# Channel stage: three images as one stationary operand on the way back from the spectra, the second parity's rows from partition 64

## The chip, the cores and the metric

The kernel runs on one core of a Trainium2 chip. The metric is the time of one execution on the device in microseconds, taken as the median of three runs. Beside the timed runs there is one execution under the hardware profiler, and all views shown come from it. Engines are named as in the profile: PE is the matrix engine (its weight loads are listed apart as PEld), DVE the vector engine, ACT the scalar engine, POOL the GpSimd engine, SP the engine whose queue issues most DMAs.

## The reference, cut to what matters

Input and output are 32 images of 192 channels of 56 x 56 float32. Four layers are added one after the other, each to the group-normalised image: an attention, a two-way scan, a shift, and a long convolution. The last two work on each channel by itself, and they are what the channel stage computes:

```python
# layer 2: each group of 4 channels is moved by whole pixels and smoothed by a 3x3 Gaussian
x = x + _L2_conv_ref(_gn(x), L2_conv_offset)
# layer 3: circular convolution by way of the spectra, with one 55x55 filter a channel
x = x + _L3_conv_ref(_gn(x), ...)

def _L3_conv_ref(x, ...):
    ...
    xf = jnp.fft.rfft2(x, s)
    kf = jnp.fft.rfft2(k[0], s)
    y = jnp.fft.irfft2(xf * kf[None], s)
    y = y[..., Kh // 2:Kh // 2 + H, Kw // 2:Kw // 2 + W]
    return y + bias * x

def _gn(v, G=32, eps=1e-5):      # 32 groups of 6 channels, per image
    ...
    return ((g - m) / jnp.sqrt(s + eps)).reshape(v.shape)
```

## The kernel before

Four stages run one after the other: the filters and their spectra (`make_filter`), the attention image by image, the scan by pairs of images, and at the end `channel_blocks`, which takes all 32 images of one channel at a time. The change lies in that last stage, in the constants that it loads, and in the place of the filter's rows in `make_filter`.

In the channel stage the 32 images stand as 16 pairs. Images of even and odd number (two "parities") are held on two ranges of partitions: a tile `x` has on partitions 0 to 56 the 56 rows, and one row of means, of the even images, on 57 to 113 those of the odd ones, and along the free dimension 16 images x 56 columns. One DMA fills it (L1582), and 15 such tiles rotate (pool `d_x`, L1477).

The groups of six channels are pipelined: while group n is shifted and centred, group n-1 goes through its spectra. For each channel these generators run, and the loop at L1719 to L1735 steps them in a fixed order written out as a tuple (L1726 to L1729):

- `shift` (L1577, two a step for the first three steps of a group): 8 matmuls with `x` as the stationary operand and the row matrix moving (L1589), DVE scales the result into `turned` (L1596), 8 matmuls with `turned` stationary and the column matrix moving (L1607), DVE adds to `x` (L1615) and sums it (L1616). The two matrices are made on POOL for four channels at a time, one of them with a matmul (L1550).
- `centre` (L1631, two a step for the last three steps): DVE subtracts the means into `padded` (L1633), ACT squares, DVE sums (L1636). `middle` and `spread` sum over the group with small matmuls (L1624).
- `analyse` (L1644): 8 matmuls with the padded rows of four images stationary (L1757), ACT copies of the result into `y` (L1763), then in three batches a real and an imaginary matmul (`re`, `im`, L1655) and six DVE operations each, which multiply by the filter's spectrum into `real` and `imag` (L1662 to L1668).
- `synthesise` (L1671): the way back. Columns first: for each of the 16 pairs `real` and then `imag` of the pair's 2 x 42 frequencies is the stationary operand (84 x 84) and the constant `f3` moves (112 columns, L1681); four pairs share a PSUM bank, and ACT copies each bank to `z` (L1688). Then rows: the constant `f4` (84 x 114) is stationary and `z` of eight pairs moves (448 columns, L1698); DVE scales by the group's deviation (L1700) and adds to `x` (L1701). Two DMAs store the channel, one for each parity (L1704). The generator yields after each bank of columns (four times) and each half of the rows (twice).

`synthesise` of channel j runs during the step of channel j+1 under the name `ending`. The tiles `ps` are four PSUM banks shared by all of this, `re` and `im` have two banks each. The instructions of an engine run in a fixed order; the order across the generators is that of the tuple, as the tile framework's scheduler leaves it. A matmul of float32 appears in the trace as two matmuls with a weight load each.

At the stage's start, DMAs bring the offsets and the constants, DVE works out the taps of all shifts from the offsets (from L1501), and POOL builds the first matrices from them.

Of the kernel before, what the change touches and what calls it, by code (L numbers as in the profile page):

```python
# [20 lines left out]
F32 = mybir.dt.float32  # L21
# [9 lines left out]
S = 56  # L31
N = S * S
# [36 lines left out]
def _resize_matrix():  # L69
# [4 lines left out]

CHANNEL = (
    (114, (2 * 2 * NF,)), (128, (2, 2 * NF)), (84, (2, 2 * S)), (84, (2, 114)), (114, (114,)), (114, (114,)),
    (114, (114,)), (112, (112,)), (114, (2,)),
)  # L80


# [39 lines left out]
def _spectral_constants():  # L122

    R = S + 1
    u, p = np.arange(NF), np.arange(S)
    turn = 2 * np.pi / PERIOD * np.outer(p, u)
    cos, sin = np.cos(turn), np.sin(turn)
    f1 = np.zeros((2, R, 2, 2, NF))
    for s in range(2):
        f1[s, :S, s, 0], f1[s, :S, s, 1] = cos, sin  # L130
# [12 lines left out]
    f4 = np.zeros((2, NF, 2, 2, R))  # L143
    for s in range(2):
        f4[s, :, 0, s, :S], f4[s, :, 1, s, :S] = weight * cos, -weight * sin
    row = np.arange(2 * R) % R
    same = np.arange(2 * R)[:, None] // R == np.arange(2 * R)[None, :] // R
    ones = np.where(same & (row[:, None] < S), 1.0 / (GROUP * N), 0.0)
    lags = np.where(row[None, :] < S, np.eye(2 * R), np.where(same & (row[:, None] < S), -1.0, 0.0))
    in_rows = same & (row[:, None] < S) & (row[None, :] < S)  # L150
    diff_y = np.where(in_rows, row[None, :] - row[:, None], 1e6)
# [3 lines left out]
    at_rows = np.stack([np.concatenate([col, [0, 0]]), row], 1)  # L155
    return {
        "f1": f1.reshape(2 * R, -1),
        "f2": f2.reshape(128, 2, -1),
        "f3": f3.reshape(2 * NF, 2, -1),
        "f4": f4.reshape(2 * NF, 2, -1),  # L160
        "ones_rows": ones,
        "lags": lags,
        "diff_y": diff_y,
        "diff_x": diff_x,
        "at_rows": at_rows,
    }
# [42 lines left out]
def make_filter(ctx: ExitStack, tc: tile.TileContext, a, consts, filt, spectra, beside):  # L209
# [84 lines left out]
        nc.sync.dma_start(out=filt[t * T : (t + 1) * T], in_=out[:, t])  # L294


    NI, PR = 16, 2 * (S + 1)
# [9 lines left out]
    for c0 in range(0, C, 2 * NI):  # L307
        t = padded[c0 // (2 * NI) % 2]
        for i in range(2):
            nc.sync.dma_start(  # L310
                out=t[(S + 1) * i : (S + 1) * i + KS, :, 0:KS],
                in_=filt[c0 + i : c0 + 2 * NI : 2].rearrange("q (a b) -> a q b", b=KS),
            )
# [12 lines left out]
        nc.sync.dma_start(out=spectra[:, c0 : c0 + 2 * NI], in_=g)  # L326
# [1136 lines left out]
def channel_blocks(ctx: ExitStack, tc: tile.TileContext, a, k, x2, rs2, spectra, out):  # L1463
# [5 lines left out]

    nc = tc.nc
    NB = out.shape[0]
    NI, NG = NB // 2, NB // 4
    PR = 2 * (S + 1)
# [25 lines left out]
    nc.vector.tensor_scalar(off, off, -(2.0**21), 2.0**21, ALU.max, ALU.min)  # L1501
    rnd = cp.tile([PR, NP, 2], F32, name="rnd", tag="rnd")
# [29 lines left out]
    def matrices(n):  # L1532
# [4 lines left out]
        for d, diff in ((1, diff_y), (0, diff_x)):  # L1537
# [9 lines left out]
            nc.gpsimd.tensor_tensor(mat, t[0], t[2], ALU.add)  # L1547
            if d == 1:
                ps = pp.tile([128, BANK], F32, name="ps", tag="ps", bufs=4)
                nc.tensor.matmul(ps[:PR, :PR], lags, mat, start=True, stop=True)  # L1550
                mat = wp.tile([r, m], F32, name="mat2", tag="mat2", bufs=3)
                nc.vector.tensor_copy(mat, ps[:PR, :PR])
            got.append(mat)
        made.clear()
        made[n] = got
# [2 lines left out]
    def psum():  # L1558
        return pp.tile([128, BANK], F32, name="ps", tag="ps", bufs=4)
# [17 lines left out]
    def shift(q, j):  # L1577

        c = q.n * GROUP + j
        rows, cols = matrices(c // 4)  # L1580
        x = xp.tile([PR, NI, S], F32, name="x", tag="x")
        nc.sync.dma_start(out=x, in_=x2[c].rearrange("s h g w -> (s h) g w"))  # L1582
        flat = x.rearrange("p g w -> p (g w)")
        turned = wp.tile([2 * S, NG, 2, S + 1], F32, name="turned", tag="turned")
        for g0 in range(0, NG, 4):
            n = min(4, NG - g0)
            ps = psum()
            for g in range(n):
                nc.tensor.matmul(  # L1589
                    ps[: 2 * S, g * PR : (g + 1) * PR],  # L1590
                    flat[:, (g0 + g) * 2 * S : (g0 + g + 1) * 2 * S],
                    rows,
                    start=True,
                    stop=True,
                )
            nc.vector.tensor_tensor(  # L1596
                turned[:, g0 : g0 + n].rearrange("p g s h -> p (g s) h"),
                ps[: 2 * S, : n * PR].rearrange("p (g h) -> p g h", h=S + 1),
                _bc(q.scale[:, j, g0 : g0 + n].rearrange("p g s -> p (g s)"), [2 * S, 2 * n, S + 1]),
                ALU.mult,  # L1600
            )
        yield
        for g0 in range(0, NG, 4):
            n = min(4, NG - g0)
            ps = psum()
            for g in range(n):
                nc.tensor.matmul(  # L1607
                    ps[:PR, g * 2 * S : (g + 1) * 2 * S],
                    turned[:, g0 + g].rearrange("p s h -> p (s h)"),
                    cols,  # L1610
                    start=True,
                    stop=True,
                )
# [57 lines left out]
    def synthesise(q, j, product):  # L1671

        c = q.n * GROUP + j
        real, imag = product
        z = wp.tile([84, NI, 2, S], F32, name="z", tag="z")
        for i0 in range(0, NI, 4):
            n = min(4, NI - i0)
            ps = psum()
            for i in range(n):
                for m, part in enumerate((real, imag)):  # L1680
                    nc.tensor.matmul(  # L1681
                        ps[:84, i * 2 * S : (i + 1) * 2 * S],
                        part[:, i0 + i].rearrange("p s u -> p (s u)"),
                        f3[:, m, :],
                        start=(m == 0),
                        stop=(m == 1),
                    )
            nc.scalar.copy(  # L1688
                z[:, i0 : i0 + n].rearrange("p g m w -> p (g m w)"), ps[:84, : n * 2 * S]
            )  # L1690
            yield
        x = q.x[j]
        for i0 in range(0, NI, 8):
            n = min(8, NI - i0)
            ps = psum()
            got = ps[:PR, : n * S].rearrange("p (g w) -> p g w", w=S)
            for m in range(2):
                nc.tensor.matmul(got, f4[:, m, :], z[:, i0 : i0 + n, m, :], start=(m == 0), stop=(m == 1))  # L1698
            o = wp.tile([PR, 8, S], F32, name="o", tag="o")[:, :n]
            nc.vector.tensor_tensor(o, got, _bc(q.rs[:, i0 : i0 + n], [PR, n, S]), ALU.mult)  # L1700
            nc.vector.tensor_tensor(x[:, i0 : i0 + n], x[:, i0 : i0 + n], o, ALU.add)  # L1701
            yield
        for s in range(2):
            nc.sync.dma_start(  # L1704
                out=out[s::2, c].rearrange("b h w -> h b w"), in_=x[(S + 1) * s : (S + 1) * s + S]
            )

    def centres(q, j):
# [187 lines left out]
```

## Time and profile before

| what | us |
|---|---|
| median of 3 runs (lowest, highest) | 12293.82 (12292.39, 12298.46) |
| the profiled execution | 12294.66 |
| its span, first to last instruction | 12292.8 |
| channel stage, first to last instruction | 8371.8 to 12292.8 |
| of 8500 to 9500: PE, DVE, ACT busy | 987.7, 869.4, 360.3 |
| L1681, columns back (`real`; `imag`): instructions, busy | 6144, 1090.9; 6144, 1089.5 |
| L1698, rows back: instructions, busy | 1536, 608.8 |
| L1607 / L1589 / L1757: instructions each | 3072 / 3072 / 3072 |
| L1624, L1550: instructions | 768, 96 |
| L1688, ACT's copies of `z`: count, busy, mean | 768, 405.6, 0.528 |
| L1700 / L1701, DVE: count, mean | 384, 0.612 / 384, 0.623 |

The busy time of a group is the union of its instructions' durations. A matmul's duration runs from its start to the modelled end of its result, and the next one begins long before that; two neighbouring groups therefore overlap, and the cost of a matmul on PE is read from the distance between starts. The wait at the start of a line stands in brackets, with what ended it.

### The profile page before, as it was taken

The numbers are of one execution on the slowest core, as the hardware profiler recorded it, in microseconds if no ns is written. First come the engines' busy times: TensorE is split into PE (matmuls) and PEld (weight loads), VectorE is DVE, ScalarE is ACT, GpSimd is POOL, SyncE is SP. The second block draws the span as 40 slices with busy tenths as digits, with TensorE's granted clock in tenths as the row PEclk, the third lists the DMA queues.
The fourth block names the chain that finished last, engine by engine and source line by source line (L and its number), as shares of the span: only waits on it lengthen the run. The fifth ranks groups of instructions, "written<-read, shape, count | busy, mean of one in ns | idle before, by whom it ended". The sixth has DMA issues, their size and how long they took to land. (4 is left out here: it accounts for less than half of the span.)

```text
span 12292.8 us, 164375 instructions
## 1 busy us (share of the span) xinstructions
PE 11329.2 (92%) x62734; PEld 7107.7 (58%) x62734; DVE 10836.4 (88%) x15489; ACT 6205.0 (50%) x11808; POOL 2250.7 (18%) x2228
## 2 busy tenths in 40 slices
PE   7999999999999999788888888888999999999999
PEld 3555555655555555333333333336777777777777
DVE  6888888888888887999999999997888888888888
ACT  3555555555555554566666666663333333333333
POOL 0000000000000000655555555551000000000000
PEclk9999999999999999999999999999999999999999
DMA  2111111111111111244344433442111111111111
GB/s 69 40 42 46 52 41 40 40 40 40 40 40 40 42 50 44 75 103 100 95 97 103 101 94 97 103 101 65 44 41 45 41 44 42 44 42 44 42 43 29
DMA packets 930055, 719.69 MB, mean 59 GB/s; under 512 B 770325, under 2 KB 807236, under 8 KB 920124
## 3 DMA queue, kind: packets, MB, share of 16 engines
q1 hardware_dynamic: 919020, 683.39, 21.7%
q10 hardware_dynamic: 10240, 25.70, 0.8%
q8 instruction: 500, 8.19, 0.3%
q14 instruction: 295, 2.42, 0.1%
HBM read 403.47 MB, written 240.65 MB: 52 GB/s over the span
## 5 line engine op out<-in xcount | busy, mean ns | idle before, releaser
L572 DVE SCALAR_TENSOR_TENSOR o<-v_a,att_w,o 128x896 f32<-128x896 f32 (+1 forms) x1024 | 1053.8, 1029 | 418.6 <-ACT v_a L546 291.5
L1763 ACT COPY y<-ps 64x252 f32<-64x252 f32 (+1 forms) x2376 | 808.2, 340 | 1135.0 <-PE ps L1757 1104.8
L1681 PE MATMUL ps<-fixed,real 84*84 84x112 f32 x6144 | 1090.9, 259 | 0.0
L1681 PE MATMUL ps<-fixed,imag 84*84 84x112 f32 x6144 | 1089.5, 259 | 0.0
L1688 ACT COPY z<-ps 84x448 f32<-84x448 f32 x768 | 405.6, 528 | 1218.5 <-PE ps L1681 1217.0
L1086 POOL MEMSET f<- 128x1 f32 x96 | 8.9, 99 | 4726.3 <-DMA st_c<-st 4721.3
L1681 PEld LDWEIGHTS ps<-fixed,real 84*84 84x84 f32 x6144 | 784.0, 153 | 134.2 <-issue 95.8
L1681 PEld LDWEIGHTS ps<-fixed,imag 84*84 84x84 f32 x6144 | 763.8, 153 | 0.0
L1079 ACT ACTIVATE q<-q 128x784 f32<-128x784 f32 x384 | 328.2, 855 | 802.5 <-DVE q L1074 633.1
L834 PE MATMUL ps<-sq,fixed 128*128 128x392 f32 x512 | 297.3, 743 | 428.6 <-ACT sq L1157 428.6
L572 DVE SCALAR_TENSOR_TENSOR o<-v_c,att_w,o 128x448 f32<-128x448 f32 (+1 forms) x1024 | 635.0, 620 | 5.1
L585 PE MATMUL ps<-xs_a,gk_a 128*98 128x448 f32 (+1 forms) x1536 | 637.1, 495 | 0.0
L589 ACT ACTIVATE pr<-ps,low 98x896 f32<-98x896 f32 (+1 forms) x384 | 352.3, 918 | 559.9 <-DVE low L587 559.9
L586 PE MATMUL ps<-xs_c,gk_c 125*98 125x448 f32 (+1 forms) x1536 | 631.6, 492 | 0.0
L1547 POOL TENSOR_TENSOR mat<-tap,tap 114x114 f32<-114x114 f32 x96 | 40.8, 425 | 3166.1 <-PE ps L1607 2313.2
L677 PE MATMUL ps<-gq_a,xs_a 128*112 128x294 f32 x1792 | 602.8, 417 | 19.2 <-DVE pq L682 19.2
L1698 PE MATMUL ps<-z,fixed 84*114 84x448 f32 x1536 | 608.8, 539 | 0.0
L834 PE MATMUL ps<-x,weights 128*128 128x392 f32 x1536 | 577.4, 519 | 27.5 <-DVE bv L1108 14.2
L678 PE MATMUL ps<-gq_c,xs_c 125*112 125x294 f32 x1792 | 594.5, 412 | 0.0
L1655 PE MATMUL re<-y,fixed 128*84 128x420 f32 (+1 forms) x1152 | 532.3, 543 | 8.7 <-ACT y L1763 7.6
L1655 PE MATMUL im<-y,fixed 128*84 128x420 f32 (+1 forms) x1152 | 526.9, 538 | 0.0
L690 ACT ACTIVATE pq<-pq 112x1176 f32<-112x1176 f32 x224 | 265.3, 1184 | 498.9 <-DVE pq L682 376.0
(367 smaller groups left out, 29245.2 us busy)
## 6 DMA issues: line engine op xcount, KB each, us to landing
x<-x SPq DMA_DIRECT2D x576, 392.0 KB
x<-x SPq DMA_DIRECT2D x512, 196.0 KB
x<-x SPq DMA_DIRECT2D x192, 399.0 KB
out_x<-x SPq DMA_DIRECT2D x384, 196.0 KB
x<-in_x SPq DMA_DIRECT2D x32, 1568.0 KB
x<-x SPq DMA_DIRECT2D x32, 1568.0 KB
x<-in_x SPq DMA_DIRECT2D x64, 392.0 KB
rd<-rd ACTq DMA_DIRECT2D x128, 196.0 KB
```

The costliest lines, as they stand in the source:

```text
L572: nc.vector.scalar_tensor_tensor(dst, tap(i), dww[:, t, i : i + 1], dst, ALU.mult, ALU.add)
L585: mm(ps[P2, h, :n], g[:, cols], xs_a[j][:, px], start=True, stop=False)
L586: mm(ps[P2, h, :n], gk_c[0:KC, 2 * j + h, cols], xs_c[j][0:KC, px], start=False, stop=True)
L589: nc.scalar.activation(pr[:, :, :n], ps[P2, :, :n], AF.Exp, bias=low[:, j, p : p + 1], accum_out=sums[:, j, p : p + 1])
L677: mm(ps[:SUB, i, :HA], xs_a[j][:, px], g, start=True, stop=False)
L678: mm(ps[:SUB, i, :HA], xs_c[j][0:KC, px], gq_c[0:KC, 2 * j + (q + i) // ns], start=False, stop=True)
L834: mm(out, aa, srcs[t][h], start=True, stop=False)
L1655: nc.tensor.matmul(ps[:, : n * 84], f2[:, i, :], y[:, i0 : i0 + n].rearrange("p g s u -> p (g s u)"), start=True, stop=True)
L1681: nc.tensor.matmul(ps[:84, i * 2 * S : (i + 1) * 2 * S], part[:, i0 + i].rearrange("p s u -> p (s u)"), f3[:, m, :], start=(m == 0), stop= ...
L1688: nc.scalar.copy(z[:, i0 : i0 + n].rearrange("p g m w -> p (g m w)"), ps[:84, : n * 2 * S])
L1698: nc.tensor.matmul(got, f4[:, m, :], z[:, i0 : i0 + n, m, :], start=(m == 0), stop=(m == 1))
L1763: nc.scalar.copy(y[64 * m : 64 * m + 64, 2 * g0 + i : 2 * (g0 + n) : 2], got[64 * i : 64 * i + 64, :, :, m, :])
```

## The change

`synthesise` now takes three images at a time as the stationary operand of the columns: `real` and `imag` are read as one run of 32 x 42 frequencies and cut into pieces of 126, ten whole ones and a last one of 84 (two images). That gives 11 x 2 matmuls in place of 16 x 2, in banks of 4, 4 and 3 pieces. `z` has 126 partitions and 11 pieces.

The rows that come next have to sort three images of a piece back to the parities. Two consecutive pieces hold six images, that is three pairs: the first pair comes from the even piece (its images 0 and 1), the third from the odd piece (its images 1 and 2), the middle pair from the even piece's last and the odd piece's first image. `f4` therefore has four blocks of columns: two of 121 columns for the first and third pairs, and two of 64 columns for the middle pair, whose two matmuls write partitions 0 to 63 and 64 to 127 of the same bank. The 16 pairs are taken as 9 and 7; the seventh of the second lot comes from the last piece alone.

For that the second parity's rows start at partition 64 instead of 57, everywhere: `PR` is 64 + 57 = 121, the constants are laid out anew, and `x` is loaded by two DMAs, one for each parity. The `x` tiles are now fixed (15 of them), cleared once in partitions 32 to 63, and so are the two `turned` tiles, whose parities lie 64 columns apart. The row matrix keeps 114 columns, so the moving operand of L1589 is as wide as before.

`synthesise` yields five times a channel instead of six.

```diff
+PR = 64 + S + 1
...
-    xp = ctx.enter_context(tc.tile_pool(name="d_x", bufs=15))
...
+    shifted = [cp.tile([PR, NI, S], F32, name=f"x{i}", tag=f"x{i}") for i in range(15)]
+    for t in shifted:
+        nc.vector.memset(t[32:64], 0.0)
+    sides = [cp.tile([2 * S, NG, 2, 64], F32, name=f"turned{i}", tag=f"turned{i}") for i in range(2)]
+    for t in sides:
+        nc.vector.memset(t[:, :, :, S + 1 : 64], 0.0)
...
-        x = xp.tile([PR, NI, S], F32, name="x", tag="x")
-        nc.sync.dma_start(out=x, in_=x2[c].rearrange("s h g w -> (s h) g w"))
+        x, turned, W = shifted[c % len(shifted)], sides[c % 2], 2 * (S + 1)
+        for s in range(2):
+            nc.sync.dma_start(out=x[64 * s : 64 * s + S + 1], in_=x2[c, s])
...
-                    turned[:, g0 + g].rearrange("p s h -> p (s h)"),
+                    turned[:, g0 + g].rearrange("p s h -> p (s h)")[:, 0:PR],
...
-        z = wp.tile([84, NI, 2, S], F32, name="z", tag="z")
-        for i0 in range(0, NI, 4):
-            n = min(4, NI - i0)
+        parts = [t.rearrange("p g s u -> p (g s u)") for t in product]
+        z = wp.tile([126, NT, 2, S], F32, name="z", tag="z")
+        for i0 in range(0, NT, 4):
+            n = min(4, NT - i0)
             ps = psum()
+            rows = []
             for i in range(n):
+                at = 126 * (i0 + i)
+                r = min(126, NB * 42 - at)
+                rows.append(r)
...
+                        ps[:r, i * 2 * S : (i + 1) * 2 * S], part[:, at : at + r], f3[:, m, :], start=(m == 0), stop=(m == 1)
...
+            full = rows.count(126)
+            for r, i, k in ((126, 0, full), (rows[-1], full, n)):
+                if i < k:
+                    nc.scalar.copy(
+                        z[:r, i0 + i : i0 + k].rearrange("p g m w -> p (g m w)"), ps[:r, i * 2 * S : k * 2 * S]
+                    )
             yield
...
-        for i0 in range(0, NI, 8):
-            n = min(8, NI - i0)
+        for p0 in range(0, NI, 9):
+            n = min(9, NI - p0)
+            k0, k = 2 * (p0 // 3), n // 3
             ps = psum()
...
+            ev, od = z[:, k0 : k0 + 2 * k : 2], z[:, k0 + 1 : k0 + 2 * k : 2]
+            if k > 0:
+                sums += [
+                    ((got[:PR, 0 : 3 * k : 3], f4[:, :, 0:PR], ev),),
+                    ((got[:PR, 2 : 3 * k : 3], f4[:, :, PR : 2 * PR], od),),
+                    (
+                        (got[0:64, 1 : 3 * k : 3], f4[:, :, 2 * PR : 2 * PR + 64], ev),
+                        (got[64:128, 1 : 3 * k : 3], f4[:, :, 2 * PR + 64 : 2 * PR + 128], od),
+                    ),
+                ]
+            left, at = n - 3 * k, k0 + 2 * k
+            if left > 0:
+                r = min(126, NB * 42 - 126 * at)
+                sums.append(((got[:PR, 3 * k : 3 * k + 1], f4[:r, :, 0:PR], z[:r, at : at + 1]),))
...
+            for beside in sums:
+                for m in range(2):
+                    for to, w, src in beside:
+                        nc.tensor.matmul(to, w[:, m], src[:, :, m], start=(m == 0), stop=(m == 1))
```

More of the change, by code (lines that the diff above doesn't have):

```diff
@@ L142, in _spectral_constants @@
     weight = np.where(u == 0, 1.0, 2.0)[:, None] / PERIOD**2
[L143 to L151, printed above, removed]
+    f4 = np.zeros((3, NF, 2, 2 * PR + 128))
+    for i, c in ((0, 0), (1, 64), (1, PR), (2, PR + 64), (2, 2 * PR), (0, 2 * PR + 64)):
+        f4[i, :, 0, c : c + S], f4[i, :, 1, c : c + S] = weight * cos, -weight * sin
+    parity, row = np.arange(PR) // 64, np.arange(PR) % 64
+    same = parity[:, None] == parity[None, :]
+    ones = np.where(same & (row[:, None] < S) & (row[None, :] <= S), 1.0 / (GROUP * N), 0.0)
+    lags = np.where(row[None, :] < S, np.eye(PR), np.where(same & (row[:, None] < S) & (row[None, :] == S), -1.0, 0.0))
+    to = np.arange(2 * R)
+    in_rows = (parity[:, None] == to[None, :] // R) & (row[:, None] < S) & (to[None, :] % R < S)
+    diff_y = np.where(in_rows, to[None, :] % R - row[:, None], 1e6)
     col = np.arange(2 * S) % S
@@ L1549, in matrices @@
                 ps = pp.tile([128, BANK], F32, name="ps", tag="ps", bufs=4)
-                nc.tensor.matmul(ps[:PR, :PR], lags, mat, start=True, stop=True)
+                nc.tensor.matmul(ps[:r, :m], lags, mat, start=True, stop=True)
                 mat = wp.tile([r, m], F32, name="mat2", tag="mat2", bufs=3)
-                nc.vector.tensor_copy(mat, ps[:PR, :PR])
+                nc.vector.tensor_copy(mat, ps[:r, :m])
             got.append(mat)
@@ L1673, in synthesise @@
         c = q.n * GROUP + j
-        real, imag = product
-        z = wp.tile([84, NI, 2, S], F32, name="z", tag="z")
-        for i0 in range(0, NI, 4):
-            n = min(4, NI - i0)
+        parts = [t.rearrange("p g s u -> p (g s u)") for t in product]
+        z = wp.tile([126, NT, 2, S], F32, name="z", tag="z")
+        for i0 in range(0, NT, 4):
+            n = min(4, NT - i0)
             ps = psum()
+            rows = []
             for i in range(n):
-                for m, part in enumerate((real, imag)):
+                at = 126 * (i0 + i)
+                r = min(126, NB * 42 - at)
+                rows.append(r)
+                for m, part in enumerate(parts):
@@ L1695, in synthesise @@
             ps = psum()
[L1696 to L1701, printed above, removed]
+            got = ps[:, : n * S].rearrange("p (g w) -> p g w", w=S)
@@ new lines, in synthesise @@
+            sums = []
+            ev, od = z[:, k0 : k0 + 2 * k : 2], z[:, k0 + 1 : k0 + 2 * k : 2]
[8 more added lines that the diff above has]
+                ]
@@ new lines, in synthesise @@
+            left, at = n - 3 * k, k0 + 2 * k
+            if left > 0:
+                r = min(126, NB * 42 - 126 * at)
+                sums.append(((got[:PR, 3 * k : 3 * k + 1], f4[:r, :, 0:PR], z[:r, at : at + 1]),))
+            if left == 2:
+                r = NB * 42 - 126 * (at + 1)
+                sums.append(
+                    (
+                        (got[0:64, 3 * k + 1 : 3 * k + 2], f4[:, :, 2 * PR : 2 * PR + 64], z[:, at : at + 1]),
+                        (got[64:128, 3 * k + 1 : 3 * k + 2], f4[:r, :, 2 * PR + 64 : 2 * PR + 128], z[:r, at + 1 : at + 2]),
+                    )
+                )
@@ L1704, in synthesise @@
             nc.sync.dma_start(
-                out=out[s::2, c].rearrange("b h w -> h b w"), in_=x[(S + 1) * s : (S + 1) * s + S]
+                out=out[s::2, c].rearrange("b h w -> h b w"), in_=x[64 * s : 64 * s + S]
             )
```

39 lines of the change are left out of this document (17 added, 22 removed).

## The prediction

> **What bounds the kernel now.** I read first the slices of the page, to see which stage the change lies in and which engine fills it.
>
> ```profile
> PE   7999999999999999788888888888999999999999
> DVE  6888888888888887999999999997888888888888
> PEclk9999999999999999999999999999999999999999
> ```
>
> The channel stage is the last 13 slices (8371.8 us to the end at 12292.8). There PE is at 9 in every slice, DVE at 8, and the granted clock stays full. A busy PE row counts pipelined matmuls, so I went on to windows over single channels (one window runs from one channel's first L1757 to the next one's; columns are length, then busy us of PE, PEld, DVE, ACT, POOL, then clock, DMA share, GB/s).
>
> ```profile
> 9720.91:9737.29 16.38, 16.17 (x101) 11.69 (x100) 14.64 (x25) 8.10 (x18) 0.00 (x0) 1.00 0.21 51
> 9656.91:9680.07 23.16, 22.93 (x167) 18.39 (x166) 19.08 (x34) 6.20 (x16) 3.21 (x6) 1.00 0.14 36
> ```
>
> Of a group's six channels, three also carry two `shift`s (about 23.2 us), three carry two `centre`s (17.6, 16.4 and 17.7 us). PE leaves 0.2 us idle. The timeline of the short channel shows what PE does with it.
>
> ```profile
> 9720.91 2.44 PE L1757 MATMUL ps<-fixed,padded 114*128 114x168 f32 x16
> 9723.56 0.94 PE L1655 MATMUL re<-y,fixed 128*84 128x420 f32 x2 [0.21 <-ACT y L1763]
> 9734.28 3.17 PE L1698 MATMUL ps<-z,fixed 84*114 84x448 f32 x8
> 9737.29 1.88 PE L1757 MATMUL ps<-fixed,padded 114*128 114x168 f32 x12
> ```
>
> Matmuls follow each other without a hole, but for a wait of some 0.4 us on ACT's copies of `y`. So what counts is not a matmul's duration (latency is in it) but its spacing, start to start. L1698: 3.01 us for 8, 0.376 each. L1757: (2.44 - 0.31)/15 = 0.142 each for 168 moving columns.
>
> ```profile
> 9665.87 0.35 PE L1681 MATMUL ps<-fixed,real 84*84 84x112 f32 x2
> ...
> 9667.98 0.35 PE L1681 MATMUL ps<-fixed,imag 84*84 84x112 f32 x2
> 10004.01 1.76 PE L1607 MATMUL ps<-mat,turned 112*114 112x112 f32 x16
> 9705.98 1.37 PE L1624 MATMUL ps<-sums,fixed 114*114 114x16 f32 x12 [0.21 <-ACT y L1763]
> ```
>
> L1681: 22 starts in 2.11 us, 0.096 each. L1607 moves the same 112 columns against 114 stationary ones instead of 84: (1.76 - 0.26)/15 = 0.100. L1624 moves only 16 against 114 and needs as long: (1.37 - 0.25)/11 = 0.10. So there are two floors, one by moving columns and one by stationary columns, and at 114 stationary ones the second gives 0.100. I take it in proportion: 0.106 at 121 columns, 0.1105 at 126.
>
> **The change, part by part.** Every matmul written is two of the trace (L1681: 32 a channel in the code, 12288 = 64 x 192 in the page).
>
> Way back, columns (L1681). 64 instructions of 0.096 are 6.14 us a channel. After it, ten threes at 126 columns are 40 instructions, the last piece (84) four: 40 x 0.1105 + 4 x 0.096 = 4.80. That is -1.34 us a channel, -257 us over 192. At 0.100 (the row of 114) it would be -338, at 0.112 (the same proportion carried to 128) -246.
>
> The Trainium skill, "TensorE: Matmul & The Clock Gate", section LDWEIGHTS, speaks against counting by matmuls saved: loading time goes with the stationary columns. It gives columns/1.2 ns, 0.095 at 114, where L1607 and L1624 show 0.100; by its figure 126 columns would be 0.105 and 121 0.101, and the whole sum, an estimate from that page, some 70 us lower than mine.
>
> Way back, rows (L1698). 8 instructions of 0.376 are 3.01 us. After it the first nine pairs take 4 instructions for the lower images and 4 for the third ones (121 stationary, 168 moving, 0.142), and 4 steps of two 64-column matmuls side by side for the middle image that straddles two threes. The second seven have 112 moving columns, where the 121 stationary ones decide: 12 x 0.106 (4 of them for the image left over) and 4 steps at 0.096. The channel stage has no such halves today; the attention stage has, and shows both gain and price.
>
> ```profile
> 2515.59 0.92 PE L544 MATMUL ps<-xs_a,att_w 128*128 128x448 f32 x2
> 2516.34 0.92 PE L545 MATMUL ps<-xs_c,att_c 65*128 65x448 f32 x2
> 2517.19 0.97 PE L551 MATMUL ps<-xs_a,att_w 128*64 128x448 f32 x4
> 2517.99 0.92 PE L553 MATMUL ps<-xs_c,att_c 65*64 65x448 f32 x4
> 2518.84 1.02 PE L834 MATMUL ps<-o,att_w 128*128 128x448 f32 x2
> ```
>
> The halves' eight matmuls take 1.65 us, four steps of 0.376 (1.50) and 0.15 more: two run side by side at the price of one. The two of L545 ahead of them take 0.85, where those of L544 take 0.75. A stretch of halves so costs 0.24 us on top. First part: 12 x 0.142 + 0.24 = 1.94; second: 12 x 0.106 + 4 x 0.096 + 0.24 = 1.90; together 3.84, +0.83 us a channel, +160 us.
>
> The Trainium skill, "TensorEngine Tiling (Array Packing)", sections Overview and Key Properties, promises up to twofold for 64 columns and says that a change of mode drains the engine, without a price. By the twofold alone, the sum would be 2 x 0.24 x 192 = 92 us lower; the row above is what the drain costs, and I keep it.
>
> Rows from partition 64. L1607's stationary operand grows from 114 to 121 columns: 16 a channel x 0.006 x 192 = +18 us. L1624: 768 x 0.006 = +5. L1589 (112 stationary) and L1757 (128) keep their columns; contracting 121 rows instead of 114 shows in no spacing (84, 112 and 128 rows all follow columns). DVE and ACT work on more partitions with as many elements, so their times stay. ACT's copies of `z` fall from 4 x 0.528 to two of those and two shorter ones; ACT is idle half the time, worth nothing. SP issues one more load a channel (0.28 us each) on a queue that is otherwise idle for most of a channel; the buffers and how far ahead they are loaded stay at 15.
>
> New clearing at the stage's start: 15 DVE memsets of 896 columns and two short ones, ahead of the offsets' arithmetic in DVE's order.
>
> ```profile
> 8374.77 0.21 DVE L1501 TENSOR_SCALAR off<-off 114x96 f32<-114x96 f32 x1 [2.89 <-DMA off<-in_L_conv_offset]
> L906 DVE MEMSET wogs<- 128x128 f32 x1 | 0.2, 165 | 0.1
> ```
>
> 128 columns take 165 ns, one column 59 (L1496), so 896 take about 0.81 us: 15 x 0.81 + 0.3 = 12.4 us, less the 2.9 in which DVE waits there anyway: +9.5 us, on the chain that builds the first matrices while PE waits. At worst 12.4, at best 0 if the first group catches up.
>
> Order. With one `yield` fewer, the first half of the rows now stands right after the columns, ahead of the second `shift` of a channel, and its two DVE operations (0.68 and 0.62) ahead of L1596 on DVE. In the order in which the changed program's instructions stand, L1607 then follows L1589 directly in the second shift channel of a group, as it does here:
>
> ```profile
> 9671.95 1.74 PE L1589 MATMUL ps<-mat,x 114*112 114x114 f32 x16
> 9672.93 0.63 DVE L1596 TENSOR_TENSOR turned<-ps,scale 112x456 f32<-112x456 f32 x1 [1.75 <-PE ps L1589]
> 9673.72 1.02 PE L1607 MATMUL ps<-mat,turned 112*114 112x112 f32 x8
> ```
>
> Today L1596 starts 0.98 us after L1589 and DVE has been idle for 1.75. After it, DVE gets the rows' result at 0.2 and is done at about 1.4; `turned` comes 0.42 us later, and PE waits for it: 0.42 x 32 groups = +13 us. In the other two shift channels a L1655 pair (0.85 or 1.7) stands between and hides it. In the centre channels DVE needs (16.06 + 14.64 + 17.20)/3 = 15.97 us of PE's 17.2; PE's 17.2 falls to about 16.7, so DVE still fits, though with 0.7 us to spare instead of 1.2.
>
> Sum: -257 + 160 + 18 + 5 + 9.5 + 13 = -51.5 us. The profiled execution took 12294.66 (span 12292.8 and 1.9 around it); 12294.7 - 51.5 = 12243, and as the median lies 0.8 lower, **12242 us** (-0.42%).
>
> **The rivals.** *Wide operands load unseen.* If 126 and 121 columns cost no more than 84, the spacing is 0.096 throughout: Z falls by another 40 x 0.0145 x 192 = 111, the rows by 12 x 0.010 x 192 = 23, the +23 vanish: 12085 us. For it: nothing beyond a queue that loads ahead. Against it: L1624, 0.10 for 16 moving columns.
>
> *DVE's idle time stays.* If DVE cannot give up its 1.2 us of idle a centre channel (in-order waits on `re`, `im` with two buffers each), the three centre channels keep their length, and 96 x 0.45 = 43 us of the gain are lost: 12285. For it: 17.20 of 17.66 busy in the third one. Against it: those windows leave 1.7 in the other two.
>
> *PE waits for DVE at every shift (slower).* Place: L1607 behind L1596, now behind the rows' two operations or a backlog of L1655's six. Price 0.58 us (a whole 1.3 us less the 0.72 that L1589 covers), twice a shift channel, 192 times: 111, less the 13 counted: 12340. It decides once L1655 no longer stands between or is itself late; a mean of 0.27 us a channel eats the whole gain. For it: L1589 waits already cost 0.2 at L1607. Against: the order above.
>
> *The halves do not run side by side.* Then 4 x 0.142 + 4 x 0.096 = 0.95 more a channel: 12425. For it: here the two read alternate threes of one tile. Against it: the row of L551.
>
> **How the numbers follow.** Forecast 0.58 (its own range 12205 to 12280: from 0.107 a wide matmul and no clearing that shows, to 0.112 and twice the waits), unseen loads 0.08, DVE's idle stays 0.16, slower 0.14, halves in turn 0.04. About 0.2% (25 us) is what a measurement of this kernel tells from no change, so faster means under 12269: 0.08 and six sevenths of the forecast, 0.58; within: the rest of it and DVE's idle, 0.24; slower 0.18. Range 12160 to 12325, which takes in the -338 of the columns: it leaves out the unseen loads, the halves in turn and part of the slower case.
>
> **What would show it.** Spacing of the 126-column matmuls near 0.110 (0.096 proves the first rival); the 64-column ones in pairs some 7 ns apart with about 0.1 us lost before and 0.15 in and after them; short channels at 15.9 and shift channels at 22.9; L1607's wait in one shift channel of three. The prediction is wrong if L1607 or L1655 wait on DVE in most channels, or if a stretch of halves costs other than 0.24.

## The result, and the profile after

| | us |
|---|---|
| before, median of 5 runs, the three above among them (lowest, highest) | 12293.82 (12292.39, 12298.80) |
| after, median of 5 runs (lowest, highest) | 12358.94 (12357.29, 12364.13) |
| ratio, with its 95% interval | 1.0052 (1.0038 to 1.0067) |
| span of the profiled execution, before and after | 12292.8 and 12357.1 |

The changed kernel is slower by 65 us, where 51.5 less were forecast, and the time lies outside the range. The first part of the page (busy us of each engine, share of the span, instructions) already says of what kind the loss is:

```profile
PE 11290.6 (91%) x64270; PEld 7234.4 (59%) x64270; DVE 10832.5 (88%) x15506; ACT 6092.2 (49%) x11808; POOL 2263.1 (18%) x2228
```

PE was busy for 11329.2 us before. It now has 39 us less to do in a span that is 64 us longer, and DVE as much as before (10836.4). So the work as a whole did not become dearer; the engines wait. The slices don't show it: their rows of PE, DVE and PEclk are the same, digit by digit. So I took the distance from one channel's first analysis matmul (L1757, now L1801) to the next one's, medians over the stage, by the place of the channel in two successive groups of six (channels 1 to 3 shift, 4 to 6 centre; channel 1 also finishes the group before):

| us | 1 | 2 | 3 | 4 | 5 | 6 | 1 | 2 | 3 | 4 | 5 | 6 |
|---|---|---|---|---|---|---|---|---|---|---|---|---|
| before | 23.03 | 23.17 | 23.26 | 17.58 | 16.38 | 17.66 | 23.25 | 23.20 | 23.22 | 17.58 | 16.38 | 17.66 |
| after | 25.22 | 23.04 | 22.79 | 17.29 | 16.01 | 17.98 | 27.09 | 22.78 | 22.77 | 17.28 | 16.01 | 17.98 |

Eight of the twelve are shorter, by 0.13 to 0.47. Channel 1 is longer by 2.19 and 3.84, channel 6 by 0.32. With 16 such pairs of groups: these eight -2.8 x 16 = -45, channel 1 +6.0 x 16 = +96, channel 6 +0.32 x 32 = +10, and the first matmul of the stage starts 9.4 later (8395.33 for 8385.97); together about +71 by medians, where the spans differ by 64. The same by windows of the changed kernel, one channel each (length, then busy us of PE, PEld, DVE, ACT, POOL, clock, DMA share, GB/s): channels 5, 6, 1 and 2.

```profile
9746.56:9762.57 16.01, 15.80 (x110) 12.29 (x110) 14.30 (x25) 6.49 (x17) 0.00 (x0) 1.00 0.21 52
9762.57:9780.56 17.99, 16.85 (x121) 13.33 (x120) 15.22 (x26) 7.44 (x18) 0.00 (x0) 1.00 0.18 46
9780.56:9807.65 27.09, 24.07 (x179) 19.46 (x178) 22.60 (x39) 6.98 (x19) 4.08 (x5) 1.00 0.15 37
9807.65:9830.43 22.78, 22.60 (x175) 18.98 (x174) 18.89 (x33) 5.64 (x16) 2.32 (x5) 1.00 0.14 37
```

In the third line PE is idle for 3.0 us, DVE for 4.5 and ACT for 20. No engine is full there; they wait for each other. The timeline of that channel's start shows in what order. (Line numbers are now those of the changed kernel: square L1647, its sum L1648, centring L1645, rows L1744 and L1745, copies of `y` L1807, small sums L1636.)

```profile
9779.45 0.67 DVE L1745 TENSOR_TENSOR x<-x,o 121x504 f32<-121x504 f32 x1
9780.05 1.08 DVE L1645 TENSOR_TENSOR padded<-x,mean 121x896 f32<-121x896 f32 x1
9780.56 1.96 PE L1801 MATMUL ps<-fixed,padded 121*128 121x168 f32 x12
...
9781.64 0.67 DVE L1675 TENSOR_TENSOR a<-im,g 84x504 f32<-84x504 f32 x1
9781.70 2.62 ACT L1807 COPY y<-ps 64x252 f32<-64x252 f32 x7 [7.14 <-PE ps L1801]
9783.24 0.84 PE L1801 MATMUL ps<-fixed,padded 121*128 121x168 f32 x4 [0.72 <-ACT y L1807]
...
9784.23 0.95 ACT L1647 ACTIVATE sq<-padded 121x896 f32<-121x896 f32 x1
...
9785.21 1.08 DVE L1648 TENSOR_REDUCE sums<-sq 121x16 f32<-121x896 f32 x1 [2.90 <-ACT sq L1647]
...
9786.21 0.93 DVE L1676 TENSOR_TENSOR real<-a,a 84x504 f32<-84x504 f32 x1
9786.35 0.38 PE L1636 MATMUL ps<-sums,fixed 121*121 121x16 f32 x2 [0.25 <-DVE sums L1648]
...
9787.07 0.67 DVE L1678 TENSOR_TENSOR a<-re,g 84x504 f32<-84x504 f32 x1
...
9787.79 0.94 PE L1667 MATMUL re<-y,fixed 128*84 128x420 f32 x2 [1.06 <-DVE a L1678]
```

The group's last centring ends at 9781.13; the rows of the channel before (L1744, L1745) now stand ahead of it on DVE. Its square could start then; ACT is idle. But in ACT's order seven copies of the next channel's `y` stand ahead of it, and the first of these starts at 9781.70, when its bank is ready. The square comes at 9784.23, the sum behind it at 9785.21 after 2.90 us in which DVE does nothing, and the products behind the sum (L1676, L1678) come as late, so that PE waits for its `re` bank. In the kernel before the same three steps lie at the end of the channel that came earlier, and the products go on:

```profile
9749.62 1.08 DVE L1633 TENSOR_TENSOR padded<-x,mean 114x896 f32<-114x896 f32 x1
...
9750.80 0.95 ACT L1635 ACTIVATE sq<-padded 114x896 f32<-114x896 f32 x1 [0.95 <-DVE padded L1633]
...
9751.78 1.09 DVE L1636 TENSOR_REDUCE sums<-sq 114x16 f32<-114x896 f32 x1
9752.78 0.67 DVE L1663 TENSOR_TENSOR a<-im,g 84x504 f32<-84x504 f32 x1
...
9754.95 2.24 PE L1757 MATMUL ps<-fixed,padded 114*128 114x168 f32 x14
...
9756.09 1.11 ACT L1763 COPY y<-ps 64x252 f32<-64x252 f32 x3 [0.43 <-PE ps L1757]
```

Channel 6 shows the same in small: two copies of `y`, then the square of a centring, then the other ten copies, on which PE waits:

```profile
9763.69 0.73 ACT L1807 COPY y<-ps 64x252 f32<-64x252 f32 x2 [6.08 <-PE ps L1801]
9764.45 0.95 ACT L1647 ACTIVATE sq<-padded 121x896 f32<-121x896 f32 x1
...
9766.22 0.94 PE L1667 MATMUL re<-y,fixed 128*84 128x420 f32 x2 [1.14 <-ACT y L1807]
```

Counted from start to start, less one spacing, the wait from L1801 to the first L1667 is 1.30 us, where the other centre channels have 0.37. The tuple in the code orders steps of generators, not instructions of ACT. With rows a step earlier and other waits in between, the scheduler left the instructions of ACT in another order; neither kernel's source says so.

### The profile page after: what moved, and what is told of

Its sections match the earlier page's. It is cut to its first block, busy times and chain, and to the rows that moved or that the text cites. A ratio compares the mean times of both kernels' runs of the same rounds, so it can differ in the third digit from the quotient of the medians.

```text
span 12357.1 us, 167701 instructions
## 1 busy us (share of the span) xinstructions
PE 11290.6 (91%) x64270; PEld 7234.4 (59%) x64270; DVE 10832.5 (88%) x15506; ACT 6092.2 (49%) x11808; POOL 2263.1 (18%) x2228
## 5 line engine op out<-in xcount | busy, mean ns | idle before, releaser
L1807 ACT COPY y<-ps 64x252 f32<-64x252 f32 (+1 forms) x2376 | 808.3, 340 | 1493.8 <-PE ps L1801 1462.5
L1703 ACT COPY z<-ps 126x448 f32<-126x448 f32 (+2 forms) x768 | 299.0, 415 | 1108.9 <-PE ps L1697 1108.2
L1697 PE MATMUL ps<-fixed,imag 84*126 84x112 f32 (+1 forms) x4224 | 803.3, 272 | 0.0
L1697 PE MATMUL ps<-fixed,real 84*126 84x112 f32 (+1 forms) x4224 | 800.2, 271 | 0.1
L1741 PE MATMUL ps<-z,fixed 126*121 126x168 f32 (+4 forms) x6912 | 792.9, 290 | 0.0
L1741 PEld LDWEIGHTS ps<-z,fixed 126*121 126x121 f32 (+2 forms) x6912 | 673.2, 163 | 167.2 <-issue 102.0
L1697 PEld LDWEIGHTS ps<-fixed,real 84*126 84x126 f32 (+1 forms) x4224 | 645.1, 187 | 100.3 <-issue 79.7
L1559 POOL TENSOR_TENSOR mat<-tap,tap 121x114 f32<-121x114 f32 x96 | 42.6, 444 | 3210.3 <-PE ps L1619 2379.6
L1697 PEld LDWEIGHTS ps<-fixed,imag 84*126 84x126 f32 (+1 forms) x4224 | 623.8, 187 | 0.4 <-DVE x L1745 0.2
L1667 PE MATMUL re<-y,fixed 128*84 128x420 f32 (+1 forms) x1152 | 541.8, 551 | 59.5 <-ACT y L1807 42.7
L1667 PE MATMUL im<-y,fixed 128*84 128x420 f32 (+1 forms) x1152 | 529.2, 541 | 0.0
```

Source lines behind the costliest of these rows:

```text
L1667: nc.tensor.matmul(ps[:, : n * 84], f2[:, i, :], y[:, i0 : i0 + n].rearrange("p g s u -> p (g s u)"), start=True, stop=True)
L1697: nc.tensor.matmul(ps[:r, i * 2 * S : (i + 1) * 2 * S], part[:, at : at + r], f3[:, m, :], start=(m == 0), stop=(m == 1))
L1741: nc.tensor.matmul(to, w[:, m], src[:, :, m], start=(m == 0), stop=(m == 1))
L1807: nc.scalar.copy(y[64 * m : 64 * m + 64, 2 * g0 + i : 2 * (g0 + n) : 2], got[64 * i : 64 * i + 64, :, :, m, :])
```

## The experiments

Theory A is throughout that the order of the instructions at the group's border makes the loss; its exact form was narrowed as runs came in. Theory B is that DVE has no room, so that a stall taken away at one place comes back at the next. Where an expectation has letters with numbers, it says what they mean. All these kernels compute the same result. An edit names one step or one edge, but the scheduler orders every engine anew after it; where the traces show that other instructions changed places too, the text says so. Ratios are to the kernel before, with 95% intervals; in brackets stand the two lengths of channel 1, medians.

**Rows back at their old step** (the `yield` that the change took out, put back):

```diff
+            yield
             yield
         x = q.x[j]
```

> The changed kernel with one more yield, so that the rows' first part stands at its old place, behind the second shift or centre of a channel; the same matmuls. Theory A (border: the last centring of a group falls behind the rows' first part on DVE and its square behind seven copies of y on ACT, DVE waits 2.9 us for it and everything of the group's first channel is late; 8.3 us in two groups): most of it comes back, 12225 to 12275 us, the group's first channel near 23 us instead of 25.2 and 27.1. Theory B (DVE is full, PE's saving can't be had in any order): 12320 to 12360. Theory C (the prices of the wide matmuls and of the halves are worse than thought, and the border is only where it shows): no change, 12350 to 12365.

12374.16 us, ratio 1.0067 (1.0050 to 1.0083) [26.16, 25.41]. No repair: more than any of the three theories expected (12365 at most). The square does come ahead of the copies now, but other instructions have changed places, as the timeline of that kernel's channel 1 shows:

```profile
9668.84 0.93 PE L1802 MATMUL ps<-fixed,padded 121*128 121x168 f32 x2 [1.58 <-ACT y L1808]
...
9669.56 0.43 PE L1636 MATMUL ps<-sums,fixed 121*121 121x16 f32 x2
...
9670.03 0.27 ACT L1653 ACTIVATE rs<-ps,eps 121x16 f32<-121x16 f32 x1 [1.25 <-PE ps L1636]
...
9675.30 0.63 DVE L1608 TENSOR_TENSOR turned<-ps,scale 112x456 f32<-112x456 f32 x1 [5.23 <-PE ps L1601]
```

PE's last small sum (L1636) now stands amid the analysis matmuls, `rs` amid the copies of `y`, and each waits for the other. Moving a step in the tuple is thus no clean way to undo the order.

**The kernel before, rows a step earlier** (one `yield` left out, nothing else):

```diff
-            yield
+            if i0 != 8:
+                yield
         x = q.x[j]
```

> The kernel before with one yield fewer, so that the rows' first half stands a step earlier as in the change; the old matmuls. In its ACT order the last square of a group stays ahead of the copies of y. Theory A in its narrow form (it is the square behind the copies that costs): 12290 to 12310 us. Its wide form (rows ahead of the last centring cost by themselves): up to 95 us more, 12370 to 12390. Theory C: no change, 12294.

12262.42 us, ratio 0.9976 (0.9966 to 0.9985) [22.78, 23.00]. The rows' new place costs nothing by itself; in the old kernel it gains some 30 us, since the waits of 0.19 from L1589 to L1607 and those among the L1757 largely go. What fails is the place together with the rest of the change.

**Clearing later** (14 of the 15 memsets of `x`, and those of `turned`, behind the arithmetic of the offsets):

> The changed kernel with 14 of the 15 clearings of x and those of turned moved behind the arithmetic on the offsets. All theories: the first matmul of the stage comes at its old time (8386 instead of 8395.3), and if that is not caught up later the time falls by 9 us, to 12350; if the first groups absorb it, 12359.

12352.34 us, ratio 1.0047 (1.0031 to 1.0064). The whole is 6.6 us shorter: the clearing is not the loss. But the first matmul starts at 8390.93, not at 8386 as expected (8395.33 in the changed kernel): in the built order six of the fourteen clearings still stand ahead of or amid the arithmetic, and eight in a row (7.39 us) ahead of DVE's first copy of a matrix. So this run does not show the whole price of the clearing.

**The last square first** (the copies of `y` of a group's first channel ordered behind the group's last square; an edge that gives an order between instructions of one engine and nothing else):

```diff
+        if j == 0:
+            for made_ in copies:
+                tc.add_manual_dep(made_.ins, q.square.ins.name, behind, ...)
```

> The changed kernel with one order edge: on ACT the copies of y of a group's first channel stand behind the last square of the group before. Nothing else is asked for. Theory A narrow: DVE's wait of 2.9 us at the border goes, about 2 to 4 us a group come back, 12240 to 12300 us. Theory A wide (the place of the rows on DVE decides): little, 12330 to 12360. Theory B: 12340 to 12360, the wait moves to another place of the same channels.

12297.53 us, ratio 1.0003 (0.9994 to 1.0013) [23.74, 24.39]; 61 us come back, as theory A narrow expected. Of the other channels only one changes by more than 0.05 us (the first channel 2, 23.04 to 22.78). The built order, compared instruction by instruction from trace to trace: in the half of the groups that lost most (channel 1 from 27.09 to 24.39) DVE's order is the same as in the changed kernel, and on PE two float32 matmuls at the border (four instructions, the last small sum and L1562) stand somewhat earlier. In the other half a dozen operations of DVE and some matmuls of channels 1 to 3 changed places too, so that there ACT's order is not the only difference.

**Spread later**, in the changed kernel, and in the kernel before: the group's small sums and `rs` asked for one channel later.

> The changed kernel with the sums and the deviation of a group (spread) asked for one channel later, when the next group's first analysis is done; its result is needed only another channel later. The last square stays behind seven copies of y. Theory A2 (the border's chain, last square to DVE's sum to L1636 to ACT's deviation, stands amid the next channel's work on three queues that go in order, and each of its links costs): most of the border goes, 12265 to 12310 us, and DVE's wait of 2.9 us for the square remains. Theory A narrow (only the square's place counts): no change, 12345 to 12365. Theory B (DVE full): 12340 to 12360.

> The kernel before with spread one channel later. Theory A2: there the chain stands wholly ahead of the next channel's analysis, and nothing waits for it; no change, 12280 to 12295 us. If it gained 30 us or more, the chain costs in both kernels and isn't what the change brought.

12350.52 us (1.0048, 1.0032 to 1.0065) [26.44, 27.97], and 12293.69 (1.0000, 0.9991 to 1.0010). Theory A2 (12265 to 12310) failed and A narrow (no change) held: the small sums and `rs`, which end the border's chain, are not what it waits for. The square with its sum is left.

**Spread later with the square first**, and the same with the 64-column steps of both row parts in one stretch:

> The changed kernel with both: spread one channel later and the copies of y behind the last square. Theory A2: all channels of a group's border like the others (22.8 us), only the fifth centre channel at 18.0; from 12358.9 less 107 us, 12245 to 12270. Theory B: not under 12300.

> The kernel of e9 with the halves of both parts of the rows in one stretch, so that one stretch's price goes (0.24 us a channel by the trace of the change: 0.09 before, 0.05 in and 0.09 after it). If PE sets the time: 0.24 x 192 = 45 us less than e9. If DVE has become the bound: 0 to 15 us less.

12307.67 (1.0012, 1.0003 to 1.0022) [25.24, 26.05], worse than the square first alone, outside A2's 12245 to 12270 and within what B allowed; and 12295.19 (1.0001, 0.9992 to 1.0011) [24.72, 25.04]. One stretch less for each channel is worth 0.24 x 192 = 46 us by its own price; 12 came. That is what was expected if DVE had become the bound, but the trace shows another wait. Channels 4 and 6 became shorter (17.28 to 16.98, 16.95 to 16.85), but channels 2 and 5 longer (22.80 to 23.28 in one group, 16.01 to 16.32), and channel 3 in the same group as that channel 2 (22.78 to 23.19). In these channels 2 and 5 PE now loses 1.07 and 1.11 us among and right behind the analysis matmuls, for 0.44 and 0.43 before, waiting for ACT's copies of `y`; DVE is idle for 4.8 and 2.0 us of them. What lengthened channel 3 stays open.

**All squares first** (the edge for the copies of every channel, behind whatever squares were asked for ahead of them):

```diff
+        last = list(squares)
+        for made_ in _rows_to_spectra(...):
+            for square in last:
+                tc.add_manual_dep(made_.ins, square.ins.name, behind, ...)
```

> The changed kernel, with an order on ACT alone: in every channel the copies of y stand behind the last square that was asked for, not only in a group's first channel (12297.5 us). Theory A (the place of the last squares in ACT's order sets both long channels): the channel of 17.98 us falls to about 17.2, the first of a group stays near 23.7 to 24.4, so 12297.5 - 0.8 x 32 = about 12272 us. Theory B (VectorE has no room left, so a stall that is taken away at one place comes back at the next): within 10 us of 12297.

12257.50 us, ratio 0.9969 (0.9957 to 0.9981) [23.38, 24.08], channel 6 at 17.00. Windows of that kernel, channels 6 and 1 (columns as above), and its ACT's timeline at the border:

```profile
9826.85:9843.85 17.00, 16.79 (x116) 12.72 (x113) 15.29 (x26) 7.45 (x18) 0.00 (x0) 1.00 0.18 42
9743.85:9767.93 24.08, 23.33 (x179) 19.39 (x178) 21.79 (x39) 6.87 (x19) 3.73 (x5) 1.00 0.16 42
```

```profile
9744.01 0.95 ACT L1649 ACTIVATE sq<-padded 121x896 f32<-121x896 f32 x1 [6.15 <-DVE padded L1647]
9744.99 3.00 ACT L1813 COPY y<-ps 64x252 f32<-64x252 f32 x8
```

The same matmuls and DVE operations are done as in the changed kernel; the edges, which name ACT's instructions alone, are worth 101 us (12358.94 - 12257.50) and turn 0.52% slower into 0.31% faster. What else changed places is what changed with the last square first, and in channel 6 one product of DVE, by two places. DVE does the same work in shorter channels, so theory B falls. The sum at the border no longer waits:

```profile
9745.02 1.07 DVE L1650 TENSOR_REDUCE sums<-sq 121x16 f32<-121x896 f32 x1
```

What is left at the border, some 0.6 and 1.3 us over the 22.8 of channel 2, are in good part waits among the L1807 of that kernel, the analysis matmuls: 1.07 us in three gaps, where other channels lose 0.06 there and 0.37 behind them. The new place of the square is not their reason: channel 1 of the changed kernel has the same 1.07, and in both kernels the first copy starts 1.14 us after the first analysis matmul. With the spread alone one channel later channel 1 loses only 0.06 in the gaps and 0.31 to 0.36 behind them, so these waits go with the place of the group's small sums; by what link was not tested.

**Centres first as well** (the second centring of a channel asked for ahead of the rows' first part), and this with the clearing later:

> As the run before, and in the three channels that centre, the second centring is asked for ahead of the rows' first part, so that its operations stand ahead of o and x on VectorE. Theory A: the first channel of a group falls from some 24 us to about 22.8 too, the other channels keep 22.8, 17.3 and 16.0; 12272 - 1.25 x 32 = about 12232 us, which is what the sum of the parts gave (12242) less the waits that were counted in it. Theory B: PE then waits for x or for the rows' result instead, 12285 us or more.

> Centres and squares first, and all but one of the clearing memsets behind the arithmetic of the offsets, which alone gave 6.6 us. Theory A: about 12225 us, 0.55% less than before the change. Theory B: 12280 us or more.

12263.81 (0.9973, 0.9962 to 0.9984) [23.38, 24.51] and 12263.23 (0.9974, 0.9965 to 0.9984). A miss for A: 12232 and 12225 were expected. An earlier centring gains nothing once the squares are first. In the changed kernel with its late squares it was not tried.

**The converse in the kernel before**: the last square behind the copies of `y`. First with its sum moving along, then with the sum held ahead of the next channel's products:

> The converse, in the kernel before the change: the last square of a group and its sum stand behind seven of the next channel's copies of y on ACT, and the group's spread stands one channel later, which alone cost nothing (12293.7 us). Theory A: the first channel of a group grows from 23.0-24.1 to 25 us or more, 12330 to 12370 us; less if the sum that moved along with the square finds VectorE idle. Theory B (the border is long because of what the change adds to VectorE and PE, not because of the order): within 15 us of 12294.

> The converse once more, in the kernel before: the group's last square behind seven copies of y on ACT as before, and now its sum held ahead of the next channel's products on VectorE, as the changed kernel has it (there the last run let it slip behind two of them, and lost only 10 us). Theory A1 (a late square costs through the sum that waits for it in VectorE's order, with the products queued behind): the first channel of a group grows by 1.5 to 3 us over 24.1, 12340 to 12390 us. Theory A2 (ACT's late square costs by itself, the sum's place is nothing): as the last run, 12304 us.

12303.90 (1.0009, 1.0000 to 1.0018) and 12306.31 (1.0008, 0.9999 to 1.0018), both [24.33, 25.02]. Both expectations of a large loss failed; the first run lies where its theory B had it (within 15 us of 12294), the second where its A2 had it (12304). Against the control with the spread alone [24.10, 24.30] the late square costs 0.2 to 0.7 us in channel 1. The timeline of the second one:

```profile
9752.25 4.23 ACT L1774 COPY y<-ps 64x252 f32<-64x252 f32 x12 [5.03 <-PE ps L1768]
...
9755.79 0.63 DVE L1597 TENSOR_TENSOR turned<-ps,scale 112x456 f32<-112x456 f32 x1 [1.22 <-PE ps L1590]
...
9756.50 0.95 ACT L1641 ACTIVATE sq<-padded 114x896 f32<-114x896 f32 x1
9756.57 1.02 PE L1608 MATMUL ps<-mat,turned 112*114 112x112 f32 x8
9757.43 0.87 PE L1664 MATMUL im<-y,fixed 128*84 128x420 f32 x2
9757.48 1.09 DVE L1644 TENSOR_REDUCE sums<-sq 114x16 f32<-114x896 f32 x1 [1.06 <-ACT sq L1641]
```

The square is as late as can be, behind all twelve copies, and the sum stands ahead of the products. But DVE is not behind here (it waits 1.22 for PE before); the sum costs it a wait of 1.06 us and not 2.90, and PE has matmuls of the shift in hand meanwhile. A late square is little loss in itself; that these are the reasons is read from the timeline alone.

**The sum later** in the changed kernel, spread one channel later, the square left behind seven copies:

> The changed kernel with the group's spread one channel later (alone 12350.5 us), the square left where it is, behind seven copies on ACT, and only the last sum of squares on VectorE asked for behind the first half of the next channel's products. Theory A1: the first channel falls from 26.4 and 28.0 us to 23.5 to 24.5, 12260 to 12300 us. Theory A2: it stays above 26, 12340 us or more.

12293.57 us, ratio 0.9998 (0.9989 to 1.0008) [23.99, 25.53], against 12350.52 with the spread alone: 57 us back, and ACT's order is, instruction by instruction, that of the run with the spread alone. Theory A1 holds for the time (12260 to 12300) and for one of the two lengths; 25.53 is a us over its 24.5. DVE's order changed in more than the sum: some operations of channels 1 to 3, and a few pairs of `re` and `im` on PE, stand elsewhere too. Its DVE at the border, where the products now follow without a hole:

```profile
9756.86 1.08 DVE L1645 TENSOR_TENSOR padded<-x,mean 121x896 f32<-121x896 f32 x1
9757.86 0.67 DVE L1681 TENSOR_TENSOR a<-re,g 84x504 f32<-84x504 f32 x1
9758.46 0.67 DVE L1682 TENSOR_TENSOR a<-im,g 84x504 f32<-84x504 f32 x1
9759.05 0.67 DVE L1685 TENSOR_TENSOR a<-re,g 84x504 f32<-84x504 f32 x1
...
9769.68 1.07 DVE L1654 TENSOR_REDUCE sums<-sq 121x16 f32<-121x896 f32 x1
```

So in the changed kernel most of the loss runs from the late square through the sum that waits for it to the products queued behind the sum on DVE. Cutting either link gives some 60 us back. In the kernel before this chain could not be made to cost much; which further difference of the two orders it needs (the rows' second part behind the sum, the copies' later start) is argued from the timelines and not shown by a run.

**The version that beats both**: all squares first, and the clearing later.

> The kernel with all squares first (12257.5 us) and fourteen of the fifteen clearing memsets, with those of turned, behind the arithmetic of the offsets, which alone gave 6.6 us: 12248 to 12254 us if the two add up, 12257 if the first group gives the gain back.

12250.88 us, ratio 0.9963 (0.9949 to 0.9977). The two gains add up: 12257.50 - 6.6 = 12250.9.

## Why the prediction was wrong, point by point

- **Columns, -1.34 us a channel: right.** The 126-column matmuls are 0.110 apart; sixteen starts of pairs run from 9569.06 to 9572.35, 3.29 / 30 = 0.1097. The first rival (0.096) is out. The Trainium skill, "TensorE: Matmul & The Clock Gate", section LDWEIGHTS, has columns/1.2 ns, from which 0.105 for 126 and 0.101 for 121 are estimates; here 0.110 and 0.106 were measured, so that the proportion to the rows of the trace was the better guide.
- **Rows, +0.83: right.** Timeline of the changed kernel's PE:

```profile
9575.23 2.04 PE L1741 MATMUL ps<-z,fixed 126*121 126x168 f32 x16
9577.19 1.83 PE L1601 MATMUL ps<-mat,x 121*112 121x114 f32 x16
...
9582.24 2.09 PE L1741 MATMUL ps<-z,fixed 126*121 126x112 f32 x20
9584.17 2.51 PE L1801 MATMUL ps<-fixed,padded 121*128 121x168 f32 x16
```

  Start to next start the two parts take 1.96 and 1.93, for 1.94 and 1.90. The 64-column matmuls start in pairs 7 ns apart, and beyond their spacings (12 x 0.142, and 12 x 0.106 + 4 x 0.096) the two parts lose 0.26 and 0.27, for 0.24 each.
- **121 stationary columns, +23 us: right in price** (L1619 and L1636 0.106 apart). **Clearing, +9.5: right in size (9.4 at the first matmul), in part by luck.** The 15 memsets take 13.97 us, 0.93 each and not 0.81; against that DVE enters the stage 1.3 us earlier than before (8370.48 for 8371.82), and from the first arithmetic to the first matmul it takes 0.9 us less (10.32 for 11.20).
- **L1607's wait, +13: wrong, and small.** Where L1619 follows L1601 directly, PE waits 0.195 us, what it waited before (0.194), not 0.42 more in one shift of three. A wait of 1.16 ahead of L1619 in every second channel 1 belongs to the border: with the squares first it is gone.
- **"Order": the step that failed.** I wrote that in the centre channels DVE "still fits, though with 0.7 us to spare", and that ACT "is idle half the time, worth nothing". The averages hold: channels 4 and 5 take 17.3 and 16.0, the shift channels 22.8, where 22.9 and 15.9 for the short one were forecast. But I walked the built order of PE and DVE in the shift channels alone. I did not walk ACT's order, nor the border, where one group's last centring, square, sum and `rs` meet the next channel's analysis. An idle engine that works in order can be late all the same: ACT was idle for 7 us, then did seven copies ahead of the one instruction on which DVE's queue hung. That was missing from the sum: 2.2 and 3.8 us in channel 1, and in channel 6 0.3 us more, where the forecast had some 0.45 less for a centre channel.
- **The rivals.** The slower one (12340) comes near to the time and is wrong in place: no shift waits longer at L1607 but that one in every second channel 1 (1.16 x 16 = 19 us). "DVE's idle stays" (12285) is out too: the centre channels 4 and 5 became shorter by 0.3 and 0.37, and channel 6 by 0.66 with the squares first. With this order mended the kernel takes 12257.5 (12250.9 with the clearing moved). The sum had 12242, and 12229 without the 13 of L1607 that did not come; the 28 us between are about the 30 ((0.6 + 1.3) x 16) that are left at the border.

## What to carry to other kernels

A sum over instructions is a forecast for the kernel without new waits; before it is believed, the built order of every in-order engine has to be walked over the places where stages of a software pipeline meet, the idle engines' orders too. Where an instruction waits, ask first what stands behind it in its own queue and then what stands ahead of its producer. When a step is moved in code that a scheduler orders, an order edge on the one instruction that matters was here the cleaner tool than another place for the step; the built order is read again after it, since the edge moved other instructions too.

## What the runs showed of the hardware that was not expected

Of the hardware itself little: the spacings and the two parts of the rows came out within 0.04 us of what the rows of the old trace gave, and only the memsets (0.93 us for 0.81) were off. Not expected was how little has to move: one square of 0.95 us, started 3.1 us after its operand was ready (9781.13 to 9784.23), and with it the order at the border, was worth 61 of the 101 us that all squares first give back. And a still later square in the kernel before cost some 10.
